# Source order on three engines in a decoder layer: a scan over time laid out as a pipeline by hand

## The chip, the cores and the metric

The kernel runs on one core of a Trainium2 chip. The metric is the device time of one execution in microseconds (us), as a median over runs. The engines are named as in the profile: PE (TensorE, matmuls), PEld (its weight loads), DVE (VectorE), ACT (ScalarE), POOL (GpSimd) and SP (SyncE, whose queue issues most DMAs).

## The reference, cut to what matters

One decoder layer on x of shape 8 x 512 x 512, all in float32. It has three parts, each followed by a residual and a layer norm:

```python
x = layernorm(x + mamba(x))              # a selective scan over 512 time steps
x = layernorm(x + cross_attention(x, ctx))   # 16 heads of 32
x = layernorm(x + experts(x))            # 32 experts, 4 per token, and a shared one
```

The change lies in the first two parts and in the router and the shared expert. The first is, for each batch entry, 1024 channels d and 16 states n:

```python
xz = layernorm(x) @ in_proj; x_main, z = split(xz)
x_main = silu(causal_conv4(x_main))
dt, Bs, Cs = split(x_main @ x_proj); dt = softplus(dt @ dt_proj + b)
h[t] = exp(A * dt[t]) * h[t-1] + dt[t] * Bs[t] * x_main[t]     # for each d, n
y[t] = sum_n h[t] * Cs[t] + x_main[t] * D
out = res_scale * (y * silu(z)) @ out_proj + x
```

## The kernel before, in words

`program` (L1433) runs three stages after each other: `layers` (L83), `experts` (L1136) and `finish` (L1388). Only `layers` is touched.

**The scan.** Each of the 8 batch entries ("batches") is cut into two chunks of 256 time steps. A chunk is worked off in 32 steps; step k takes one block of 128 channels (8 blocks, two to a pair) and one group of 4 of the 16 states. So there are 64 steps a batch and 512 in all. A step does this:

- `carry` (L448, ACT): takes an `h` tile of 128 x 4 x 257 from a ring of four and copies the last state of the chunk before into its first column (L452).
- `decays` (L442, ACT): four exponentials into one of two `da` tiles (L446). They are issued one step ahead.
- `scan` (L455, DVE): the product dt·x·B into `h` (L458), the scan itself (L462), and in the first chunk a copy of the last state (L464).
- `collect` (L466): the product of `h` with C on DVE (L479), and four matmuls on PE (L483) that sum the states into `py`; the first group of a block adds x·D by two more matmuls (L471). There is one `py` tile (pool `psy`, one buffer), which holds a pair of blocks.
- `gated` (L491, DVE): every eighth step, multiplies a finished `py` by silu(z) (L495).

B and C are spread over partitions by DMAs (`bcast`, L380) from a scratch tensor, dt and dt·x by DMAs in `prepare` (L393).

**Side work.** Between the steps the loop issues other work. The front of the next chunk: `load_x`, `norm_x`, `flip_x`, `convolve` (L320), `x_proj` (L365), `gate_x` (L353), and `prepare` for each pair. The back of the last chunk: `twice_x` (L497) and `back` (L502, two halves of matmuls with out_proj, then a layer norm). And the attention, router and shared expert of the batch before: `units` (L715) and `sources` (L663) give a list of small pieces with weights in us, and the loop takes from the list in step with a planned budget (`work`, L1023). A piece issues its PE work and returns its consumers as a function; `do` (L1014) issues a piece and then, by `settle` (L1005), the consumers of the piece before; `dry` issues all that are left. The attention's pieces are `maximum` (score product, then the reduce `mx` on DVE, L777), `weigh` (score product, then an exponential on ACT, L805) and `gather` (L817). Score products share two PSUM buffers (pool `pss`), nearly all other PE results two more (pool `psm`, tag `mm`).

**What sets the order.** The source gives an order, but a list scheduler lays out each engine's instructions anew, by its own estimates of time, wherever dependences allow. It holds for all engines; only the silu calls and their table loads are held in program order (L359).

Of the kernel before, what the change touches and what calls it, by code (L numbers as in the profile page):

```python
# [8 lines left out]
F32 = mybir.dt.float32  # L9
# [3 lines left out]
ALU = mybir.AluOpType  # L13
# [4 lines left out]
P = 128  # L18
# [6 lines left out]
NST = 16  # L25
RANK = 32
CC = DI // P
T = 256
NT_ = T // P
NG = 4  # L30
HP = P // 2
# [51 lines left out]
def layers(ctx, tc, a, x1d, filld, based, xbuf):  # L83
# [23 lines left out]
    nc = tc.nc  # L107
# [11 lines left out]
    psy = ctx.enter_context(tc.tile_pool(name="l_psy", bufs=1, space=PSUM))  # L119
# [239 lines left out]
    def silu(*tiles):  # L359

        for v in tiles:
            tc.keep_in_program_order(nc.scalar.activation(v, v, AF.Silu))
        tc.keep_in_program_order(nc.scalar.preload_act_table_set(LN_EXP))
# [78 lines left out]
    def decays(c, g, dt, da):  # L442

        for n in range(NG):
            j, m = n // 2, n % 2
            nc.scalar.activation(da[:, n, 1:], dt[:, c % 2, j, :], AF.Exp, scale=aneg[:, c, j, g, m : m + 1])  # L446

    def carry(t, c, g):  # L448

        last = state[:, c, g].unsqueeze(2)  # L450
        h = mp.tile([P, NG, T + 1], F32, tag="h", name="h", bufs=4)
        nc.scalar.copy(h[:, :, 0:1], last if t else nothing)  # L452
        return h
# [9 lines left out]
        if t < S // T - 1:  # L463
            nc.vector.tensor_copy(state[:, c, g].unsqueeze(2), h[:, :, T : T + 1])  # L464

    def collect(c, g, h, bc, py, f):  # L466


        if g == 0:
            for j in range(2):  # L470
                nc.tensor.matmul(  # L471
                    py[j * HP : (j + 1) * HP, c % 2, :],
                    ident[:, j * HP : (j + 1) * HP],
                    f["xs"][c // 2][:, c % 2, :],
                    start=(c % 2 == 0),
                    stop=False,
                )
        steps = h.rearrange("p (j m) t -> p j m t", j=2)[:, :, :, 1:]
        nc.vector.tensor_tensor(steps, steps, bc[1], ALU.mult)  # L479
        for m in range(NG // 2):  # L480
            for j in range(2):
                s = (g, m, c % 2)
                nc.tensor.matmul(  # L483
                    py[j * HP : (j + 1) * HP, c % 2, :],
                    twice,
                    h[:, j * 2 + m, 1:],
                    start=False,
                    stop=(s == (NST // NG - 1, NG // 2 - 1, 1)),
                )

    def gated(q, f, py):  # L491

        f["xs"].pop(q)
        pair = f["zs"][:, 2 * q : 2 * q + 2, :]
        nc.vector.tensor_tensor(pair, pair, py, ALU.mult)  # L495

    def twice_x(b, t, f):  # L497
        f["o"] = o = mp.tile([P, NT_, D], F32, tag="xt", name="o")
        nc.sync.dma_start(o, a["x"][b, t * T : (t + 1) * T, :].rearrange("(j p) d -> p j d", p=P))
        nc.scalar.mul(o, o, 2.0)  # L500
# [31 lines left out]
    def load(name):  # L532
        loaded[name] = w = p2.tile([P, DC, D], F32, tag="wa", name="wa")
        nc.sync.dma_start(w, rows(a[name]))
# [479 lines left out]
    def do(fn, *args, first=False):  # L1014

        if first:
            dry()
        rest = fn(*args)
        settle()
        if rest:  # L1020
            left.append(rest)

    def work(k):  # L1023

        front = 6.9 if k in (1, 2) else 3.4 if 3 <= k < 7 or k in (12, 15, 18, 21, 24) else 1.0 if k in (11, 26) else 0.0
        return 1.2 + front

    f = {"xt": x0}
# [12 lines left out]
    bc, n = bcast(f, 0), 0  # L1041
    nc.scalar.activation(aneg, aneg, AF.Exp)
    nc.vector.tensor_scalar(aneg, aneg, -1.0, None, ALU.mult)
    decays(0, 0, f["ready", 0][0], das[0])
    old, side, cleared = None, [], 0

    for i, (b, t) in enumerate(chunks):
        nf = {}
        after = chunks[i + 1] if i + 1 < len(chunks) else None
        if t == 0:  # L1050
            side, spent = units(b - 1) if b else sources(0), 0.0

            own = [work(k) for k in range(len(steps))] * 2
            whole = sum(own) + sum(x[0] for x in side)
        py = None
        for k, (q, g, ci) in enumerate(steps):
            if ci == 0:
                if (q, g) != (CC // 2 - 1, NST // NG - 1):
                    bcn = bcast(f, (g + 1) % (NST // NG))
                else:  # L1060
                    bcn = bcast(nf, 0) if after else None
            h = carry(t, 2 * q + ci, g)

            if k + 1 < len(steps) or after:
                nq, ng, ni = steps[(k + 1) % len(steps)]
                decays(2 * nq + ni, ng, (f if k + 1 < len(steps) else nf)["ready", nq][0], das[(n + 1) % 2])
            scan(t, 2 * q + ci, g, f["ready", q][1], bc, das[n % 2], h)
            n += 1
            if k % 8 == 0:
                if k:  # L1070
                    gated(q - 1, f, py)
                elif old:
                    gated(CC // 2 - 1, old[2], old[3])
                py = psy.tile([P, 2, T], F32, tag="py", name="py")
            if i == 0 and k == 0:
                load("Wo")
            if i == 0 and k == 2:
                biases()
            if k == 0 and old:
                twice_x(*old[:3])  # L1080
            if k in (1, 2) and old:
                do(back, k - 1, *old[:3], first=True)
            if 3 <= k < 7:
                do(gate_x, k - 3, f, first=(k == 3))
            if k == 7:
                dry()
                silu(f["zs"])
            if k % 8 == 3:
                if q + 1 < CC // 2:
                    do(prepare, q + 1, f)  # L1090
                elif after:
                    do(prepare, 0, nf)
            if after:
                if k == 5:
                    load_x(*after, nf)
                if k == 9:
                    norm_x(nf)
                if k == 11:
                    for j in range(DC // 2):
                        do(flip_x, j, nf)  # L1100
                if k in (12, 15, 18, 21):
                    do(convolve, after[1], (k - 12) // 3, nf, first=(k == 12))
                if k == 23:
                    dry()
                    silu(*nf["xs"].values())
                if k == 24:
                    do(x_proj, nf)
            if side and (k >= 3 or t and k == 0):
                at = t * len(steps) + k + 1
                while side and spent + sum(own[:at]) <= whole * at / len(own):  # L1110
                    w, fn, alone = side.pop(0)
                    spent += w
                    do(fn, first=alone)
            settle()
            collect(2 * q + ci, g, h, bc, py, f)
            if ci == 1:
                bc = bcn
            while i < 2 and cleared < E * (i * len(steps) + k - 6) // (2 * len(steps) - 7):
                clear(cleared)
                cleared += 1  # L1120
        while t and side:
            _, fn, alone = side.pop(0)
            do(fn, first=alone)
        old = (b, t, f, py)
        f = nf
    gated(CC // 2 - 1, old[2], old[3])
    twice_x(*old[:3])
    for j in range(2):
        do(back, j, *old[:3], first=True)
    dry()  # L1130
    for _, fn, alone in units(B - 1):
        do(fn, first=alone)
# [300 lines left out]
def program(tc, a, out):  # L1433
    nc = tc.nc
    with tc.tile_pool(name="dram", bufs=1, space=DRAM) as dram:
        x1d = dram.tile([N, D], F32, name="x1d")
        filld = dram.tile([B, S], F32, name="filld")

        based = dram.tile([N + P, D], F32, name="based")
        xbuf = dram.tile([SLOTS, ROW], F32, name="xbuf")  # L1440
        nc.scalar.preload_act_table_set(LN_EXP)

        with ExitStack() as ctx:
            layers(ctx, tc, a, x1d, filld, based, xbuf)
        with ExitStack() as ctx:
            experts(ctx, tc, a, xbuf, based)
        with ExitStack() as ctx:
            finish(ctx, tc, based, out)
# [31 lines left out]
```

## Time and profile before

| | us |
|---|---|
| median of 3 runs | 5548.85 (5548.56 to 5548.85) |
| the profiled execution | 5555.79 |
| its span, first to last instruction | 5554.1 |
| busy in the span: PE, DVE, ACT | 4883.9, 4349.2, 2592.8 |
| first scan of the kernel, last scan | 56.6, 3680.6 |
| batch 0 (its 64 steps) | 365.2 |
| batches 1 to 6, each | 466.6 to 470.2 |
| from the last scan to the experts' first product | 268 |
| experts, finish | 1533, 70 |

The span is that of one execution under the profiler; the median is of executions that were only timed. The profile's columns: busy time is the time in which an engine has an instruction at work; "idle before" is the idle time just ahead of an instruction, and the name behind the arrow is what ended it. A line number is that of the kernel before. PE counts are of the profile's records, two for each float32 matmul of the source. The whole page has a view of the chain that ended last; here it shows only the last 100 us, the experts' last write and `finish`, and says nothing on the stage in question.

### The profile page before, as it was taken

The page shows a single profiled execution, that of the slowest core. Times are in us where ns is not written, and L with a number is a line of the kernel's source. Part 1 is how long each engine was busy: PE and PEld are TensorE (multiplying, and loading weights), DVE is VectorE, ACT ScalarE, POOL GpSimd, SP SyncE. Part 2 cuts the span into 40 slices and gives each one's busy share as a digit, 9 for nine tenths or more (in the row PEclk, how much of TensorE's full clock was granted, in tenths as well). Part 3 has the DMA queues.
Part 4 walks back from the last instruction along what each step waited for, and adds up shares of the span by engine and source line. Part 5 has one row for each costly group of instructions (what it writes and reads, how often), then busy time and mean ns, then how long its engine had stood idle before and what let it go on. Part 6 is the DMA issues. An engine that isn't in the chain of part 4 may idle for free. (4 is left out here: it accounts for less than half of the span.)

```text
span 5554.1 us, 60352 instructions
## 1 busy us (share of the span) xinstructions
PE 4883.9 (88%) x19752; PEld 2720.5 (49%) x19752; DVE 4349.2 (78%) x5738; ACT 2592.8 (47%) x5483; POOL 560.9 (10%) x424
## 2 busy tenths in 40 slices
PE   6768889888988988888888898879899999999994
PEld 3334344334434434443443343333577777777773
DVE  7998989989889989899989999864466565555554
ACT  5554565655556555555555655523222222222223
POOL 1000002002000200200010020010111111111111
PEclk7878999999999999999999999989999999999997
DMA  6887345445534634544463464441345444454444
GB/s 183 246 239 203 108 130 184 114 120 154 167 104 113 203 92 129 184 123 113 124 199 104 114 193 110 113 157 44 102 121 125 125 125 124 121 126 124 115 121 146
DMA packets 554282, 769.83 MB, mean 139 GB/s; under 512 B 135754, under 2 KB 268394, under 8 KB 551920
## 3 DMA queue, kind: packets, MB, share of 16 engines
q1 hardware_dynamic: 517952, 677.55, 41.5%
q0 software_dynamic: 33280, 76.90, 7.3%
q10 hardware_dynamic: 2736, 11.54, 0.5%
q8 instruction: 156, 2.56, 0.2%
q14 instruction: 158, 1.29, 0.1%
HBM read 508.68 MB, written 165.05 MB: 121 GB/s over the span
## 5 line engine op out<-in xcount | busy, mean ns | idle before, releaser
L446 ACT ACTIVATE l_da<-both,l_aneg 128x256 f32<-128x256 f32 x2048 | 888.7, 499 | 791.5 <-DVE h L462 744.2
L462 DVE TENSOR_TENSOR_SCAN h<-l_da,h 128x1028 f32<-128x1028 f32 x512 | 1169.4, 2291 | 49.9 <-ACT h L452 27.3
L483 PE MATMUL py<-h,l_twice 128*64 128x256 f32 x4096 | 632.0, 424 | 194.2 <-DVE h L479 194.0
L458 DVE TENSOR_TENSOR h<-both,bc 128x1024 f32<-128x1024 f32 x512 | 617.5, 1213 | 141.8 <-PE py L483 78.2
L479 DVE TENSOR_TENSOR h<-h,bc 128x1024 f32<-128x1024 f32 x512 | 621.9, 1218 | 6.3 <-DMA l_qa<-l_ka 0.3
L483 PEld LDWEIGHTS py<-h,l_twice 128*64 128x64 f32 x4096 | 295.2, 148 | 570.5 <-issue 246.4
L775 PE MATMUL ps_s<-l_ka,l_qa 64*128 64x512 f32 x1024 | 315.2, 695 | 141.9 <-DVE mx L777 141.4
L1230 PE MATMUL ps_h<-xT,w 128*128 128x320 f32 x1536 | 435.6, 433 | 0.0
L1310 POOL DMA_INDIRECT based<-y,xe x160 | 251.2, 1570 | 1313.4 <-ACT y L1333 573.4
L1251 DVE TENSOR_TENSOR hT<-ps_h,p 128x320 f32<-128x320 f32 x128 | 62.9, 491 | 379.1 <-PE ps_h L1230 379.1
L777 DVE TENSOR_REDUCE mx<-ps_s 128x2 f32<-128x1024 f32 x256 | 310.2, 1215 | 56.2 <-PE ps_s L775 55.5
L1230 PEld LDWEIGHTS ps_h<-xT,w 128*128 128x128 f32 x1536 | 292.2, 190 | 118.2 <-issue 0.4
L801 PE MATMUL ps_t<-l_qa,l_ka 64*128 64x512 f32 x1024 | 300.6, 651 | 15.0 <-ACT eT L805 11.4
L805 ACT ACTIVATE eT<-ps_t 128x1024 f32<-128x1024 f32 x256 | 258.7, 1012 | 109.2 <-PE ps_t L801 108.7
L817 PE MATMUL po<-eT,l_va 128*64 128x512 f32 x1024 | 281.5, 628 | 24.6 <-ACT raw L829 20.8
L650 POOL DMA_INDIRECT xbuf<-x2t,dest x128 | 218.7, 1708 | 815.8 <-DVE dest L644 777.4
L1230 PE MATMUL ps_h<-t,s 128*128 128x320 f32 x1024 | 286.1, 432 | 0.0
L712 PE MATMUL ps_p<-x2T,wa 128*128 128x512 f32 x512 | 247.5, 633 | 11.8 <-DVE hT L892 10.3
L311 PE MATMUL ps_z<-xnT,wm 128*128 128x256 f32 x1024 | 241.0, 389 | 17.8 <-DVE o L521 17.0
L311 PE MATMUL ps_x<-xnT,wm 128*128 128x256 f32 x1024 | 242.5, 390 | 2.9 <-DMA wm<-in_in_proj_w 2.0
L512 PE MATMUL po<-wm,zs 128*128 128x512 f32 x512 | 234.6, 608 | 3.9 <-DMA wm<-in_out_proj_w 1.8
L1230 PEld LDWEIGHTS ps_h<-t,s 128*128 128x128 f32 x1024 | 194.6, 190 | 81.1
(234 smaller groups left out, 7414.6 us busy)
## 6 DMA issues: line engine op xcount, KB each, us to landing
bc<-scr SPq DMA_DIRECT2D x1024, 128.0 KB
w<-in_w SPq DMA_DIRECT2D x93, 1024.0 KB
wm<-in_in_proj_w SPq DMA_DIRECT2D x128, 512.0 KB
xbuf<-zero SPq DMA_DIRECT2D x32, 1362.5 KB
xe<-xbuf SPq DMA_DIRECT2D x32, 1362.5 KB
both<-dt SPq DMA_DIRECT2D x256, 128.0 KB
both<-dtx SPq DMA_DIRECT2D x256, 128.0 KB
wm<-in_out_proj_w SPq DMA_DIRECT2D x64, 512.0 KB
```

The source lines that it names most:

```text
L311: nc.tensor.matmul(ps[:, i, :], w[:, dc, i * P : (i + 1) * P], f["xnT"][:, dc, :], start=(dc == 0), stop=(dc == DC - 1),)
L446: nc.scalar.activation(da[:, n, 1:], dt[:, c % 2, j, :], AF.Exp, scale=aneg[:, c, j, g, m : m + 1])
L458: nc.vector.tensor_tensor(steps, dtx[:, c % 2].unsqueeze(2).to_broadcast([P, 2, NG // 2, T]), bc[0], ALU.mult)
L462: nc.vector.tensor_tensor_scan(flat, da.rearrange("p n t -> p (n t)"), flat, 0.0, ALU.mult, ALU.add)
L479: nc.vector.tensor_tensor(steps, steps, bc[1], ALU.mult)
L483: nc.tensor.matmul(py[j * HP : (j + 1) * HP, c % 2, :], twice, h[:, j * 2 + m, 1:], start=False, stop=(s == (NST // NG - 1, NG // 2 - 1, 1)),)
L775: nc.tensor.matmul(ps[:, j, :], qa[r, lt * P : (lt + 1) * P], ka[r, :], start=True, stop=True)
L777: return lambda: nc.vector.tensor_reduce(mx[:, lt, :].unsqueeze(2), ps, AX.X, ALU.max) and None
L801: nc.tensor.matmul(ps[:, j, :], ka[r, kc * P : (kc + 1) * P], qa[r, :], start=True, stop=True)
L805: nc.scalar.activation(eT, ps, AF.Exp)
L817: nc.tensor.matmul(po[j * 2 * HD : (j + 1) * 2 * HD, :], va[:, kc, i, j * HD : (j + 2) * HD], eT[:, j, :], start=(kc == 0), stop=(kc == SC ...
L1230: nc.tensor.matmul(ps, w[:, n, r * P : (r + 1) * P], x[:, n, :], start=not more and n == 0, stop=n == 1, skip_group_check=more,)
```

## The change

It does four things, all in `layers`.

1. `manual_schedule` for ACT, DVE and PE: inside `layers` these three engines keep the order of the source. POOL and SP, and with SP the DMAs, are still laid out by the scheduler. 
2. `collect` keeps only the DVE product with C. Its matmuls become a function, `products`, which the loop calls at the end of the next step. `py` is taken in `products`, and `gated` moves from step k % 8 == 0 to k % 8 == 1.
3. `carry` for step k+1 is issued in step k, ahead of the decays for step k+1.
4. A `settle()` stands right after each step's scan, so that a consumer left over from one step follows the next step's scan. It replaces the one before `collect`. `back`, `gate_x` and the silu of z move one step later, and `work`'s budget with them.

```diff
-    def collect(c, g, h, bc, py, f):
-        if g == 0:
-            for j in range(2):
-                nc.tensor.matmul(py[...], ident[...], f["xs"][c // 2][:, c % 2, :], ...)
+    def collect(c, g, h, bc, f):
         steps = h.rearrange("p (j m) t -> p j m t", j=2)[:, :, :, 1:]
         nc.vector.tensor_tensor(steps, steps, bc[1], ALU.mult)
-        for m in range(NG // 2):
-            ...
+        xs = f["xs"][c // 2]
+        def products():
+            if g == 0 and c % 2 == 0:
+                f["py"] = psy.tile([P, 2, T], F32, tag="py", name="py")
+            py = f["py"]
+            ...
+        return products
...
     decays(0, 0, f["ready", 0][0], das[0])
+    ahead, products = carry(0, 0, 0), None
...
-            h = carry(t, 2 * q + ci, g)
+            h = ahead
             if k + 1 < len(steps) or after:
                 nq, ng, ni = steps[(k + 1) % len(steps)]
+                ahead = carry(t if k + 1 < len(steps) else after[1], 2 * nq + ni, ng)
                 decays(...)
             scan(t, 2 * q + ci, g, f["ready", q][1], bc, das[n % 2], h)
             n += 1
-            if k % 8 == 0:
-                if k:
-                    gated(q - 1, f, py)
+            if k % 8 == 1:
+                if k > 1:
+                    gated(q - 1, f)
                 elif old:
-                    gated(CC // 2 - 1, old[2], old[3])
-                py = psy.tile([P, 2, T], F32, tag="py", name="py")
+                    gated(CC // 2 - 1, old[2])
...
             if k == 0 and old:
-                twice_x(*old[:3])
-            if k in (1, 2) and old:
-                do(back, k - 1, *old[:3], first=True)
-            if 3 <= k < 7:
-                do(gate_x, k - 3, f, first=(k == 3))
-            if k == 7:
+                twice_x(*old)
+            settle()
+            if k in (2, 3) and old:
+                do(back, k - 2, *old, first=True)
+            if 4 <= k < 8:
+                do(gate_x, k - 4, f, first=(k == 4))
+            if k == 8:
                 dry()
                 silu(f["zs"])
...
-            if side and (k >= 3 or t and k == 0):
+            if side and (k >= 4 or t and k < 2):
...
-            settle()
-            collect(2 * q + ci, g, h, bc, py, f)
+            if products:
+                products()
+            products = collect(2 * q + ci, g, h, bc, f)
...
         with ExitStack() as ctx:
+            ctx.enter_context(tc.manual_schedule(engines={mybir.EngineType.Activation, mybir.EngineType.DVE, mybir.EngineType.PE}))
             layers(ctx, tc, a, x1d, filld, based, xbuf)
```

More of the change, by code (lines that the diff above doesn't have):

```diff
@@ L464, in scan, with gated @@
             nc.vector.tensor_copy(state[:, c, g].unsqueeze(2), h[:, :, T : T + 1])
-    def collect(c, g, h, bc, py, f):
-        if g == 0:
-            for j in range(2):
[L471 to L477, printed above, removed]
+    def collect(c, g, h, bc, f):
         steps = h.rearrange("p (j m) t -> p j m t", j=2)[:, :, :, 1:]
         nc.vector.tensor_tensor(steps, steps, bc[1], ALU.mult)
-        for m in range(NG // 2):
[L481 to L491, printed above, removed]
+        xs = f["xs"][c // 2]
[3 more added lines that the diff above has]
+            py = f["py"]
+            if g == 0:
+                for j in range(2):
+                    nc.tensor.matmul(
+                        py[j * HP : (j + 1) * HP, c % 2, :],
+                        ident[:, j * HP : (j + 1) * HP],
+                        xs[:, c % 2, :],
+                        start=(c % 2 == 0),
+                        stop=False,
+                    )
+            for m in range(NG // 2):
+                for j in range(2):
+                    s = (g, m, c % 2)
+                    nc.tensor.matmul(
+                        py[j * HP : (j + 1) * HP, c % 2, :],
+                        twice,
+                        h[:, j * 2 + m, 1:],
+                        start=False,
+                        stop=(s == (NST // NG - 1, NG // 2 - 1, 1)),
+                    )
+        return products
+    def gated(q, f):
         f["xs"].pop(q)
         pair = f["zs"][:, 2 * q : 2 * q + 2, :]
-        nc.vector.tensor_tensor(pair, pair, py, ALU.mult)
+        nc.vector.tensor_tensor(pair, pair, f["py"], ALU.mult)
     def twice_x(b, t, f):
@@ L1023, in work @@
     def work(k):
-        front = 6.9 if k in (1, 2) else 3.4 if 3 <= k < 7 or k in (12, 15, 18, 21, 24) else 1.0 if k in (11, 26) else 0.0
+        front = 6.9 if k in (2, 3) else 3.4 if 4 <= k < 8 or k in (12, 15, 18, 21, 24) else 1.0 if k in (11, 26) else 0.0
         return 1.2 + front
@@ L1054, in layers @@
             whole = sum(own) + sum(x[0] for x in side)
-        py = None
         for k, (q, g, ci) in enumerate(steps):
@@ L1123, in layers @@
             do(fn, first=alone)
-        old = (b, t, f, py)
+        old = (b, t, f)
         f = nf
-    gated(CC // 2 - 1, old[2], old[3])
-    twice_x(*old[:3])
+    products()
+    gated(CC // 2 - 1, old[2])
+    twice_x(*old)
     for j in range(2):
-        do(back, j, *old[:3], first=True)
+        do(back, j, *old, first=True)
     dry()
```

## The prediction

> **What bounds the kernel now.** I read three views, in this order. First the busy time by stage, cut at the first scan of a batch (times from the timeline). The columns are the stretch, its length, then the busy time of PE, its weight loads, DVE, ACT and POOL with their counts, the granted clock, the DMA share and GB/s.
>
> ```profile
> 56.60:421.80 365.20, 243.50 (x990) 127.11 (x988) 343.31 (x350) 198.61 (x466) 20.98 (x12) 0.76 0.81 237
> 1359.00:1827.40 468.40, 412.26 (x1685) 194.71 (x1684) 425.99 (x500) 267.87 (x564) 41.86 (x29) 0.94 0.48 138
> 3233.10:3683.00 449.90, 386.93 (x1580) 177.41 (x1579) 402.25 (x432) 241.45 (x516) 34.09 (x21) 0.93 0.46 134
> 3683.00:3951.00 268.00, 226.99 (x735) 92.80 (x736) 106.67 (x207) 65.51 (x86) 31.84 (x35) 0.89 0.33 113
> 3951.00:5484.00 1533.00, 1532.31 (x6259) 1131.45 (x6257) 895.15 (x1609) 425.52 (x929) 246.59 (x157) 1.00 0.47 116
> ```
>
> These are batch 0, batch 3 (batches 1 to 6 all take 467 to 470), batch 7, the last attention unit alone, and the experts. The change touches all but the last. In batch 3 DVE is busy for 426.0 of 468.4 us (91%) and PE for 412.3 (88%): two engines close together, and only 42.4 us of DVE idle that any order of instructions could win back. Second, DVE's groups in batch 3, with the idle time ahead of each and what ended it.
>
> ```profile
> L462 DVE TENSOR_TENSOR_SCAN h<-l_da,h 128x1028 f32<-128x1028 f32 x64 | 146.5, 2292 | 6.6 <-ACT h L452 3.8 <-ACT l_da L446 0.7
> L479 DVE TENSOR_TENSOR h<-h,bc 128x1024 f32<-128x1024 f32 x64 | 77.9, 1219 | 0.9
> L458 DVE TENSOR_TENSOR h<-both,bc 128x1024 f32<-128x1024 f32 x64 | 77.4, 1213 | 18.4 <-PE py L483 11.1 <-DMA both<-dtx 7.3
> L777 DVE TENSOR_REDUCE mx<-ps_s 128x2 f32<-128x1024 f32 x32 | 38.7, 1214 | 2.1 <-PE ps_s L775 2.0
> L345 DVE SCALAR_TENSOR_TENSOR xs<-xp,l_cw,xs 128x256 f32<-128x256 f32 x48 | 20.6, 479 | 5.5 <-ACT xs L337 5.2
> ```
>
> The three instructions of a step cost 4.7 us; 64 steps give 302 of the 426 us. The named waits are small and spread out: an h buffer not yet free (11.1), a copied dt late (7.3), a convolution (5.5). Third, the timeline of DVE, for what lies between two instructions (start, duration).
>
> ```profile
> 3560.15 2.30 DVE L462 TENSOR_TENSOR_SCAN h<-l_da,h 128x1028 f32<-128x1028 f32 x1
> 3562.49 1.23 DVE L479 TENSOR_TENSOR h<-h,bc 128x1024 f32<-128x1024 f32 x1
> 3563.63 1.22 DVE L777 TENSOR_REDUCE mx<-ps_s 128x2 f32<-128x1024 f32 x1
> 3564.76 0.68 DVE L418 SCALAR_TENSOR_TENSOR dtx<-dtx,u 128x512 f32<-128x512 f32 x1
> ```
>
> L479 reads what the scan wrote and starts 0.04 after the scan's end. L777 needs nothing of L479 and starts 0.09 before its end. Over all neighbours in the trace less than 0.35 us apart, an independent one starts 0.081 us before the end (median), a dependent one 0.034 after it, and a scan straight after its own product L458 0.103 after. So which instructions are neighbours has a price.
>
> [...]
>
> **The change, part by part.** All per batch of 64 steps, against batch 3.
>
> *Source order on DVE.* It removes no instruction: both built programs have 498 a batch, whose mean durations sum to 450.4 us. Before, 144 of the neighbours are dependent: 34 are pairs of taps, which overlap all the same, 21 are product and scan, 89 others. 450.4 − 388×0.081 + 21×0.103 + 89×0.034 = 424.2, against 426.0 measured, so the counting holds. After, the built order has 288: product, scan and copy now always stand together. 40 pairs of taps and 7 of reduces overlap; 64 are product and scan; 177 others: 450.4 − 257×0.081 + 64×0.103 + 177×0.034 = 442.2. So **+18 us on the engine that sets the pace**. What the source order may still lose to waits before it is slower: 468.4 − 442.2 = 26 us, 0.41 us a step.
>
> *Products a step later, carries a step sooner.* PE no longer stands behind the DVE product of its own step (10.1 us of PE's idle time in this batch). The carry of step k+1 needs the products of step k−3, which PE issues in step k−2, with four h buffers as before; so the 11.1 us at L458 and most of the 6.6 at the scan go. A carry that still waits for PE now holds up, behind it in ACT's queue, the four decays of that step and every evacuation after them, and so PE's next buffers; with a step and a half of slack I cost that at nothing, and at up to 3 us a batch around `back` if the slack is gone. `gated` waits for the products of the step before and holds PE's next products until it is done: counted in the next item. Next late is whatever consumer waits for PE.
>
> *Consumers behind the next scan.* I laid PE's and DVE's sums of each step (built order times the durations above) side by side. With PE's side work due 1.2 us before DVE ends the step, its products waiting for DVE's previous step, and for `gated` every eighth (one py buffer), PE is late by **12 us** in all, mostly around `back` (two pieces of some 7 us in steps 2 and 3); without any lateness 0, with PE never ahead of the scan 27.
>
> *Reduces.* Seven steps hold two neighbouring `mx` reduces with a `weigh` between their products. The two score buffers then alternate, so the second product waits for the first reduce, and DVE for it: in the tail the trace shows this gap as 1.42 us. Before, the scheduler put other work there (2.1 us in all). 7×1.42 = **10 us**; low 3 if PE finds the other buffer, high 13.
>
> *Chains across engines in one step*, which the scheduler filled: norm, transposes, shared hidden product, projection and taps in steps 52 to 54 (PE's three pieces, 3.5+3.5+3.1, end some 5 us after DVE wants the taps); `prepare` at step 11 (1.5); the second `output` (1.5); x1 fetched row block by row block in step 13 (3). Sum **11 us**; low 3, high 20, as the trace doesn't show this order.
>
> *DMAs.* SP's and POOL's queues aren't in the manual schedule; SP's order changes with the simulated one, the count (3189) doesn't; the loads of B and C wait there for the collecting product, which ends its step as before. `prepare` now stands five steps before its use; of 7.3 us of dt waits I keep **2** (0 to 9).
>
> *ACT.* Table loads fall from 18 to 10 a batch, 8×1.283 = 10 us; but ACT is busy 268 of 468 and works a step ahead, so nothing on the path. If ACT became late it would cost at most these 10 back.
>
> Sum: 442 + 12 + 10 + 11 + 2 = 477, of which I take off 1 for lateness counted twice: **476, +7.6 us a batch**, 46 for batches 1 to 6. Batch 0 has no attention: the same counting gives a floor of 363.5 where it was 341.6, and I leave it 12 of its 22 idle us (DMA share 0.81 there): 376, +11 (the biases' matmuls of step 2, now in DVE's order, are some 3 of these). Batch 7 and the last unit together: +6 (its floor is up 18 too; the unit alone has PE in the same forced order, 85% busy, and DVE at 40%; hence nothing). Experts and finish: their sources and built order are unchanged, 0. Sum +63. The profiled execution took 5555.79 (span 5554.1), the median is 5548.85, 0.12% below; the sum on the median gives **5612**.
>
> **Rivals.**
>
> *The pipeline works (ends faster).* One mechanism: PE has a step's lead (its side work of step k may start after the products of step k−2, some 3.5 us before DVE's consumers of step k), and this covers reduces and chains too. Then a batch takes 442 + 12 + 2 = 456: 7×(−12) and nothing for batch 0 gives **5465**. For it: named waits at L458 go, ACT is ahead. Against it: 26 us is all there is, and pairs of reduces can't be covered with two buffers. It decides where waits are under 0.41 us a step.
>
> *Step by step.* PE's lead is eaten by its buffers (two mm, two score, one py), so each step costs the larger of PE's and DVE's sums: these maxima sum to 475, and reduces and chains come on top, 21: 496 a batch, 7×28 + 15 gives **5760**. For it: PE 88% busy. Against: ACT frees most mm buffers early.
>
> *They cancel.* 468 to 470 a batch, **5550**. That the change doesn't do what it says is excluded: the built order shows it.
>
> **How the numbers follow.** Forecast 0.53, faster rival 0.26, step by step 0.12, cancelling 0.09. The forecast's own range, with the bounds of reduces, chains and DMA (−19 to +19 a batch about 476, not all at one end), is 5540 to 5690. For 8 in 10 I take 5465 to 5725. 0.2% (11 us) is about what a measurement of this kernel can tell from no change. Faster by more: 0.27; within: 0.08; slower: 0.65.
>
> **What would show it.** DVE busy in a batch near 442, against 426: then the counting of neighbours is right. DVE waits at `mx` near 10 us a batch with PE's score product as releaser; waits at L458 for `py` near nothing; table loads 10 a batch; a wait for taps or x2 around steps 52 to 54. A batch under 460 makes me wrong on the waits; one over 490 says PE sets the pace.

## The result, and the profile after

The changed kernel takes 5966.6 us (5961.25 to 5970.12, four runs) against 5548.85: ratio 1.075, 95% interval 1.0731 to 1.0769. The forecast had the sign and the place, but a seventh of the size: +63 us forecast, +418 measured. The time lies outside the range.

First the same stages as before, cut at the first scan of batches 0, 3 and 7, at the last scan, and at the experts' first product (columns: stretch, length, busy time of PE, PEld, DVE, ACT, POOL, granted clock, DMA share, GB/s).

```profile
57.10:449.10 392.00, 252.21 (x1010) 138.21 (x1012) 362.39 (x355) 194.42 (x468) 5.12 (x12) 0.76 0.72 213
1498.20:2023.90 525.70, 428.92 (x1684) 200.91 (x1684) 440.38 (x498) 258.04 (x556) 29.51 (x30) 0.88 0.42 124
3600.80:4101.00 500.20, 404.32 (x1584) 184.27 (x1584) 421.01 (x457) 235.35 (x509) 24.00 (x20) 0.88 0.41 119
4101.00:4368.00 267.00, 218.67 (x725) 89.86 (x726) 105.12 (x185) 67.65 (x89) 24.22 (x27) 0.89 0.31 103
```

From first scan to first scan, batch 0 takes 392.0 us (365.2 before), batches 1 to 6 523 to 526 (467 to 470), batch 7 497.8 to its last scan (447.4); what follows the last scan takes 1866.9 (1873.5). So +27, +340, +50 and -7, which is the 411 by which the spans differ (5965.5 against 5554.1). Batch 3 shows two things at once. DVE's busy time rose by 14.4 us for the same 498 instructions, the way the counting of neighbours had it (+18). And its idle time doubled, from 42.4 to 85.3 us, where it was to fall to 34. PE's idle time rose with it, from 56 to 97 us.

DVE's groups in batch 3 (instructions, busy time and mean, idle time just ahead and what ended it):

```profile
L462 DVE TENSOR_TENSOR_SCAN h<-l_da,h 128x1028 f32<-128x1028 f32 x64 | 147.2, 2300 | 6.6 <-ACT l_da L446 1.6
L469 DVE TENSOR_TENSOR h<-h,bc 128x1024 f32<-128x1024 f32 x64 | 78.0, 1218 | 0.6
L458 DVE TENSOR_TENSOR h<-both,bc 128x1024 f32<-128x1024 f32 x64 | 77.9, 1217 | 0.0
L785 DVE TENSOR_REDUCE mx<-ps_s 128x2 f32<-128x1024 f32 x32 | 38.8, 1217 | 15.8 <-PE ps_s L783 15.8
L345 DVE SCALAR_TENSOR_TENSOR xs<-xp,l_cw,xs 128x256 f32<-128x256 f32 x48 | 22.5, 482 | 14.8 <-ACT xs L337 13.6
```

The scan's own three instructions run as long as before, and L458, with 18.4 us of idle time ahead of it before, has none. That part of the pipeline works. (Of the 6.6 us ahead of L462, 1.6 are a wait; the rest is the small gap of some 0.08 us between L458 and the scan that depends on it, in each of 64 steps.) What waits now is the side work. DVE's waits in the same batch (us in total, times, longest):

```profile
DVE mx L785 <- PE ps_s L783: 15.8, 11, 3.8
DVE o L529 <- PE po L520: 14.8, 4, 7.2
DVE xs L345 <- ACT xs L337: 13.6, 3, 8.6
DVE dtx L418 <- ACT dtx L414: 9.5, 5, 3.4
DVE total L856 <- ACT r L855: 7.0, 2, 6.5
DVE zs L503 <- PE py L489: 3.6, 1, 3.6
```

None of these lines is the scan, whose one wait for decays is 1.6 us. Each is a consumer that stands at a fixed place in DVE's order, while its operand comes late from PE or ACT. (L785 is L777 of before, L529 is `norm`, L418 `prepare`, L856 the sum of `output`, L503 `gated`.) PE stands in the same way, in the same batch:

```profile
PE ps_tr L886 <- ACT x2t L80: 13.8, 1, 13.8
PE ps_p L720 <- DVE attT L858: 11.1, 1, 11.1
PE ps_t L809 <- DVE mx L785: 10.2, 3, 3.6
PE py L479 <- ACT l_da L446: 8.9, 1, 8.9
```

One account serves for all that follows. I split DVE's time in batch 3 into the durations of its 498 instructions, the sum of the small gaps between neighbours (under 0.35 us; negative where neighbours overlap), and the longer gaps, called waits.

| batch 3, us | length | durations | small gaps | waits |
|---|---|---|---|---|
| before | 468.4 | 454.0 | -22.4 | 36.8 |
| after | 525.7 | 456.0 | -2.9 | 72.6 |
| difference | +57.3 | +2.0 | +19.5 | +35.8 |

The forecast had +18 for neighbours, and 35 for all waits (12 for PE's lateness, 10 for reduces, 11 for chains, 2 for DMAs), about what the kernel before has. So the first difference is right, and the waits are twice what was forecast. The level that the forecast built on was low as well: its 442.2 us for durations and small gaps compares with 456.0 - 2.9 = 453.1, and the 424.2 of before with 454.0 - 22.4 = 431.6. The prediction took its 424.2 as confirmed by the 426.0 of busy time, but busy time leaves out the short idle gaps that the counting holds.

### The profile page after: what moved, and what is told of

Same layout as the page of the kernel before. It is cut to its first block, busy times and chain, and to the rows that moved or that the text cites. A ratio compares the mean times of both kernels' runs of the same rounds, so it can differ in the third digit from the quotient of the medians.

```text
span 5965.5 us, 60313 instructions
## 1 busy us (share of the span) xinstructions
PE 4998.5 (84%) x19752; PEld 2763.4 (46%) x19752; DVE 4468.2 (75%) x5738; ACT 2521.8 (42%) x5428; POOL 485.6 (8%) x424
## 5 line engine op out<-in xcount | busy, mean ns | idle before, releaser
L462 DVE TENSOR_TENSOR_SCAN h<-l_da,h 128x1028 f32<-128x1028 f32 x512 | 1177.3, 2299 | 56.2 <-ACT l_da L446 14.8
L446 ACT ACTIVATE l_da<-both,l_aneg 128x256 f32<-128x256 f32 x2048 | 872.4, 498 | 444.7 <-DVE h L462 442.4
L489 PE MATMUL py<-h,l_twice 128*64 128x256 f32 x4096 | 617.8, 425 | 128.5 <-DVE h L469 128.4
L469 DVE TENSOR_TENSOR h<-h,bc 128x1024 f32<-128x1024 f32 x512 | 624.0, 1219 | 5.6
L458 DVE TENSOR_TENSOR h<-both,bc 128x1024 f32<-128x1024 f32 x512 | 623.4, 1218 | 6.4 <-DMA bc<-scr 6.4
L489 PEld LDWEIGHTS py<-h,l_twice 128*64 128x64 f32 x4096 | 288.7, 148 | 495.3 <-issue 215.2
L785 DVE TENSOR_REDUCE mx<-ps_s 128x2 f32<-128x1024 f32 x256 | 310.1, 1217 | 151.8 <-PE ps_s L783 151.6
L825 PE MATMUL po<-eT,l_va 128*64 128x512 f32 x1024 | 288.9, 644 | 22.4 <-ACT raw L837 17.9
L720 PE MATMUL ps_p<-x2T,wa 128*128 128x512 f32 x512 | 286.9, 717 | 12.7 <-DVE hT L900 8.0
L311 PE MATMUL ps_z<-xnT,wm 128*128 128x256 f32 x1024 | 256.2, 407 | 25.2 <-ACT dt L409 16.9
L345 DVE SCALAR_TENSOR_TENSOR xs<-xp,l_cw,xs 128x256 f32<-128x256 f32 x384 | 180.0, 482 | 108.9 <-ACT xs L337 99.2
L658 POOL DMA_INDIRECT xbuf<-x2t,dest x128 | 180.6, 1411 | 899.5 <-DVE dest L652 356.7
L311 PE MATMUL ps_x<-xnT,wm 128*128 128x256 f32 x1024 | 247.4, 396 | 0.6 <-ACT xnT L300 0.5
L311 PEld LDWEIGHTS ps_z<-xnT,wm 128*128 128x128 f32 x1024 | 202.3, 203 | 82.0 <-ACT dt L409 21.0
```

The source lines that it names most:

```text
L311: nc.tensor.matmul(ps[:, i, :], w[:, dc, i * P : (i + 1) * P], f["xnT"][:, dc, :], start=(dc == 0), stop=(dc == DC - 1),)
L458: nc.vector.tensor_tensor(steps, dtx[:, c % 2].unsqueeze(2).to_broadcast([P, 2, NG // 2, T]), bc[0], ALU.mult)
L462: nc.vector.tensor_tensor_scan(flat, da.rearrange("p n t -> p (n t)"), flat, 0.0, ALU.mult, ALU.add)
L489: nc.tensor.matmul(py[j * HP : (j + 1) * HP, c % 2, :], twice, h[:, j * 2 + m, 1:], start=False, stop=(s == (NST // NG - 1, NG // 2 - 1, 1)),)
L720: nc.tensor.matmul(ps, lhs(dc), rhs(dc), start=(dc == 0), stop=(dc == DC - 1))
L785: return lambda: nc.vector.tensor_reduce(mx[:, lt, :].unsqueeze(2), ps, AX.X, ALU.max) and None
```

## The experiments

My theory after the result: a few late places (`back`, the reduces, `prepare`, the taps) hold DVE, and each can be mended alone. The rival: orders fixed on DVE and on PE make the two stand at each other by turns, so that mending one place moves the wait to the next. A third: the layout is itself worse, whoever orders it. The kernel before, timed again with each group of experiments, had medians from 5549 to 5557 us, so a difference of less than some 10 us between two experiments says nothing by itself. Every kernel is the changed one with the edit shown, unless said otherwise; ratios are to the kernel before, with 95% intervals; "waits" and "small gaps" are those of batch 3 as above.

**The layout without the fixed order, and the fixed order without the layout.**

```diff
-            ctx.enter_context(tc.manual_schedule(engines={Activation, DVE, PE}))   # e1: taken out
```

> The changed source without the manual schedule: the list scheduler lays out all engines again. If in-order waits on DVE and adjacent dependent neighbours are the cause (+36 and +20 us in a batch of 526), both go and a batch takes 460 to 475, in all 5500 to 5600 us. If it is the reshaped source itself (products a step later, work shifted), it stays over 5800.

```diff
+            ctx.enter_context(tc.manual_schedule(engines={Activation, DVE, PE}))   # e2: put into the kernel before
```

> The source of before with the manual schedule alone, products and consumers in the same step. In-order waits: DVE's product with C is now followed by consumers with no scan between, PE has no step of lead, so slower than the changed kernel, 6200 to 6800 us. If the reshaping did nothing for the in-order engines, it is within 1% of 5967.

Measured: 5607.5 us, 1.0097 (1.0077 to 1.0116), for the layout alone, and 6660.1 us, 1.1991 (1.1971 to 1.2011), for the fixed order alone. In batch 3 the layout under the scheduler has small gaps of -21.1 and waits of 43.4; the fixed order of the old source -2.3 and 166.8. So the layout does what it is laid out for: it takes 694 us off a kernel whose engines keep the source's order. But it doesn't pay for that order: under the scheduler it costs 1% rather than gain, and the fixed order costs 359 us more.

**Which engine's order.**

```diff
-            ctx.enter_context(tc.manual_schedule(engines={Activation, DVE, PE}))
+            ctx.enter_context(tc.manual_schedule(engines={DVE}))   # e3; e4 {Activation, PE}; e16 {PE}; e17 {Activation}; e18 {DVE, PE}
```

> Changed source, only DVE in source order, PE and ACT by the scheduler. If DVE's own order is the cause, nearly all of the loss stays: 5850 to 6000 us. If PE's order sets the pace, it falls to 5600 to 5700.

> Changed source, ACT and PE in source order, DVE by the scheduler. If DVE's own order is the cause: 5550 to 5700 us, with overlap of neighbours back near -22 us a batch and waits below 50. If PE's order sets the pace, 5850 to 6000.

> Changed source, PE alone in source order, ACT and DVE by the scheduler. With ACT and PE in order it was 5821, with none 5607. If PE's order is what blocks, 5750 to 5820; if ACT's (decays behind evacuations that wait for PE), 5620 to 5680.

> The changed source with only ACT in the order of the source. If each fixed order costs by itself and the three overlap (5607 with none, 5777 with PE alone, 5859 with DVE alone, 5821 with ACT and PE, 5967 with all), ACT alone costs about the difference between ACT with PE and PE alone, 44: 5650 (5620 to 5680). If ACT's queue is what ties DVE to PE (a carry that waits for PE holds up the decays behind it), ACT alone costs most of what two engines cost: over 5730.

> The changed source with DVE and PE in the order of the source and ACT laid out by the scheduler. If the loss lies between DVE and PE and ACT only adds its own small share, 5920 (5890 to 5950), all but some 45 of the whole. If ACT's fixed order is what ties the two together, the time falls near that of DVE alone, below 5870.

| engines in the source's order | us | ratio | small gaps | waits | PE idle |
|---|---|---|---|---|---|
| none (e1) | 5607.5 | 1.0097 (1.0077 to 1.0116) | -21.1 | 43.4 | 64.0 |
| ACT (e17) | 5658.2 | 1.0191 (1.0174 to 1.0208) | -25.8 | 56.3 | 57.9 |
| PE (e16) | 5777.1 | 1.0392 (1.0375 to 1.0410) | -19.6 | 64.3 | 84.5 |
| ACT, PE (e4) | 5820.8 | 1.0474 (1.0452 to 1.0495) | -22.5 | 71.2 | 89.2 |
| DVE (e3) | 5859.1 | 1.0552 (1.0534 to 1.0571) | -4.6 | 59.2 | 87.3 |
| DVE, PE (e18) | 5961.4 | 1.0736 (1.0719 to 1.0754) | -3.8 | 70.0 | 100.9 |
| all (after) | 5966.6 | 1.0750 (1.0731 to 1.0769) | -2.9 | 72.6 | 96.8 |

The small gaps close only where DVE is in order, by 16.5 us a batch for DVE alone: that is the neighbours' price by itself. The waits grow with any of the engines. With DVE and PE fixed the time is that of all three within some 5 us: ACT's order adds nothing to theirs, and my e18 forecast (ACT adds some 45) was too high for ACT. But the loss doesn't need both. DVE alone costs 252 us over e1 and PE alone 170, which sum to more than the 354 of the two together; so the costs overlap, and each order makes waits even where the other engine is free (59.2 and 64.3, from 43.4). Neither of e4's branches came true (5821, between them). Where the waits stand depends on which order is fixed. With PE alone fixed, the scheduler lets DVE run ahead until it needs an h buffer that PE has not yet read:

```profile
DVE h L458 <- PE py L489: 35.9, 13, 13.4
```

With DVE fixed as well this line is gone, and DVE stands at the side work instead:

```profile
DVE xs L345 <- ACT xs L337: 18.4, 5, 9.9
DVE o L529 <- PE po L520: 13.2, 4, 7.2
DVE dtx L418 <- ACT dtx L414: 12.9, 3, 4.5
DVE mx L785 <- PE ps_s L783: 7.5, 7, 1.6
```

**The neighbours alone.** DVE's product with C of step k-1 is put between L458 and the scan of step k, so that the scan no longer stands right behind the product that it reads, nor the product with C right behind its scan.

```diff
-    def scan(t, c, g, dtx, bc, da, h):
+    def scan(t, c, g, dtx, bc, da, h, between=None):
...
+        if between:
+            between()
...
-            scan(t, 2 * q + ci, g, f["ready", q][1], bc, das[n % 2], h)
+            scan(t, 2 * q + ci, g, f["ready", q][1], bc, das[n % 2], h, weighted)
```

> Changed kernel with DVE's product with C of step k-1 put between the product and the scan of step k, so that no scan stands straight behind its own product. Neighbour theory: 64 pairs become independent, 64 x 0.184 = 12 us a batch plus up to 5 where collect stood behind its scan; waits unchanged; 90 to 130 us faster, near 5860. If neighbours cost nothing[...], 5967 within 20.

Measured: 5906.5 us, 1.0637 (1.0620 to 1.0655). Small gaps fall from -2.9 to -14.5, waits stay (74.9). The timeline shows where (start, duration):

```profile
1722.26 1.22 DVE L458 TENSOR_TENSOR h<-both,bc 128x1024 f32<-128x1024 f32 x1
1723.39 1.22 DVE L474 TENSOR_TENSOR h<-h,bc 128x1024 f32<-128x1024 f32 x1
1724.53 2.29 DVE L464 TENSOR_TENSOR_SCAN h<-l_da,h 128x1028 f32<-128x1028 f32 x1
```

L474 (the product with C) starts 0.09 us before L458 ends, and the scan 0.08 before L474 ends. In the changed kernel the scan stands right behind its own product and starts 0.10 after its end, while an instruction of other data behind the scan starts 0.07 before its end:

```profile
2006.26 1.22 DVE L458 TENSOR_TENSOR h<-both,bc 128x1024 f32<-128x1024 f32 x1
2007.58 2.30 DVE L462 TENSOR_TENSOR_SCAN h<-l_da,h 128x1028 f32<-128x1028 f32 x1
2009.81 0.66 DVE L914 TENSOR_TENSOR z<-ps_p,x2t 128x512 f32<-128x512 f32 x1
```

So an exchange of neighbours alone gives back 60 us of the 418. The small gaps gained what was forecast (11.6 us a batch, of 12); the time gained less (60 us, of 90 to 130).

**Mending single places.** `prepare` a step later (e5); the other taps of a convolution one `settle` later (e6); the fourth convolution a step sooner (e12); `gated` ahead of its step's product and scan (e10).

```diff
-            if k % 8 == 3:
+            if k % 8 == 4:  # e5
...
-            return other_taps
+            return lambda: other_taps            # e6
...
-                if k in (12, 15, 18, 21):
-                    do(convolve, after[1], (k - 12) // 3, nf, first=(k == 12))
+                if k in (12, 15, 18, 20):        # e12
+                    do(convolve, after[1], (k - 11) // 3, nf, first=(k == 12))
...
-            scan(t, 2 * q + ci, g, f["ready", q][1], bc, das[n % 2], h)     # e10: moved
-            n += 1
             if k % 8 == 1:
                 ...
+            scan(t, 2 * q + ci, g, f["ready", q][1], bc, das[n % 2], h)
+            n += 1
```

> Changed kernel with prepare one step later (k % 8 == 4), so that at steps 3 and 35 the norm of back no longer has to run before prepare's matmuls, but follows the next scan. If the waits come from the distance between producer and consumer in the source: the 15 us a batch ahead of L529 fall to below 5, and the kernel gains 50 to 90 us. If PE's pace costs the time, the wait reappears behind other consumers and the kernel stays within 20 us of 5967.

> Changed kernel with the convolution's other taps issued one piece later. Distance theory: of 13.6 us a batch ahead of L345 (4.2 at step 16, 8.6 at step 54) most goes, 50 to 90 us in all. PE's pace: within 20 us of 5967.

> Changed kernel with the fourth convolution of the next chunk at k = 20 instead of 21, so that at step 52 its projection stands ahead of the transposes of x2 in PE's queue, where they wait 13.8 us for the layer norm. Head-of-line theory: the 8.6 us ahead of the taps at step 54 fall below 2, 30 to 50 us in all. If PE's work alone counts, the wait reappears at the router's or another consumer and the gain is under 15 us.

> Changed kernel with gated ahead of its step's product and scan instead of behind them (still k % 8 == 1), so that the one py buffer comes free 3.5 us sooner. Head-of-line theory: PE idles 8.9 us at step 1 behind the first products of a new pair, with back's ready matmuls queued behind them; the same at each of 8 pairs a batch. Then waits ahead of L529 fall by 3 to 7 us a batch, and all by 8 to 15: 60 to 110 us faster. If PE's total work sets the pace, or py comes free in time, within 20 us of 5967.

Measured: 5945.0 us, 1.0707 (1.0689 to 1.0725), for e5; 5968.0, 1.0746 (1.0728 to 1.0764), for e6; 5963.3, 1.0740 (1.0722 to 1.0757), for e12; 6029.8, 1.0859 (1.0841 to 1.0877), for e10. Only e5 gains, by 22 us, where 50 to 90 were forecast if single places were at fault. e6 says nothing: the taps stayed the first work behind the scan, with the same wait of 8.6 us at step 54. In e12 that wait is gone, others of 7.6 and 5.0 us for the same operand stand at steps 20 and 52, and the waits ahead of the taps are longer in all (13.6 in the changed kernel):

```profile
DVE xs L345 <- ACT xs L337: 17.8, 3, 7.6
```

At `mx` they are shorter (15.8 to 7.6), so that all waits come to 69.7. In e5 the 14.8 us ahead of L529 fall to 5.2, and those ahead of L418 rise from 9.5 to 20.7:

```profile
DVE dtx L418 <- ACT dtx L414: 20.7, 7, 6.2
...
DVE o L529 <- PE po L520: 5.2, 4, 2.3
```

The place for e10 I took from the timeline of the changed kernel, around the first `gated` of a chunk:

```profile
1505.66 0.68 DVE L503 TENSOR_TENSOR zs<-zs,py 128x512 f32<-128x512 f32 x1
...
1506.49 1.12 PE L479 MATMUL py<-xs,l_ident 128*64 128x256 f32 x4 [8.94 <-ACT l_da L446]
...
1507.37 1.95 PE L489 MATMUL py<-h,l_twice 128*64 128x256 f32 x8
...
1509.24 7.30 PE L520 MATMUL po<-wm,zs 128*128 128x512 f32 x16
...
1523.38 0.75 DVE L529 SCALAR_TENSOR_TENSOR o<-po,l_rs,o 128x512 f32<-128x512 f32 x1 [7.16 <-PE po L520]
```

PE is idle for 8.94 us and starts again 0.15 after `gated` has ended (the single `py` must be read first; the decay that the profile names as releaser ends at that moment, but these matmuls don't read it). Behind it stand both halves of `back`, 7.3 and 7.1 us, and at their end DVE, at `norm`, for 7.16. With `gated` sooner, DVE waits less at L529 but stands at `gated` for the last products:

```profile
DVE zs L503 <- PE py L489: 18.6, 5, 7.3
...
DVE o L529 <- PE po L520: 10.6, 4, 4.6
```

15.0 us more there against 4.2 less, and the kernel is 63 us slower where 60 to 110 were to be gained. In e5 and e10 the wait that grew is that of the very piece that the edit moved, so these two show that a place can't be shifted for nothing, not that a wait wanders elsewhere. Last, e9, e10 and e12 together (their three edits in one):

> Interleaved product with C, gate first and project first together. Head-of-line theory: the gains add, 60 + 60 to 110 + 40: 5750 to 5810 us, still slower than before. If the waits only move about, 5880 to 5910, the interleaving alone.

Measured: 6058.5 us, 1.0905 (1.0887 to 1.0924). Small gaps stay mended (-14.4), and waits are 97.8: more than with any of the three alone (74.9, 77.7 and 69.7), and 25 more than in the changed kernel, where the three changes taken singly sum to some 5. So places can't be mended one by one and their gains added. That some choice of mends helps is not excluded: e10 was already a loss by itself, and e5, which gained, was not in this kernel.

**Less work for PE.** Every second matmul with `twice` (L489) is left out, so half of the states are missing from y.

```diff
-            for m in range(NG // 2):
+            for m in (NG // 2 - 1,):
```

> Changed kernel that leaves out half of the py matmuls (two of four in each step, so half of the states are missing from y). It takes some 0.6 us of PE work out of each step, 36 us a batch, and leaves DVE's and ACT's order. If PE's pace sets the time: 250 to 300 us faster, near 5700. If it is the latency of chains at some places: under 120 us, at 5850 or above.

Measured: 5870.3 us, 1.0570 (1.0552 to 1.0587). PE's busy time in batch 3 falls by 29.9 us (428.9 to 399.1), and the batch by 14.0. A microsecond of PE work is worth about half a microsecond, so PE isn't the bound by its sum; its idle time rose to 112.7.

**The distance of products and carries.** The products in their own step again (e19, e19b), two steps later (e21, with the gate, `back` and `gate_x` one step later too), and the carry in its own step (e20).

```diff
-            if products:
-                products()
-            products = collect(2 * q + ci, g, h, bc, f)
+            collect(2 * q + ci, g, h, bc, f)()                      # e19, e19b
...
+            if len(products) == 2:                                  # e21
+                products.pop(0)()
+            products.append(collect(2 * q + ci, g, h, bc, f))
...
-            h = ahead
+            h = carry(t, 2 * q + ci, g)                             # e20
...
-                ahead = carry(t if k + 1 < len(steps) else after[1], 2 * nq + ni, ng)
```

> The changed kernel with one of its parts undone: the products follow their own step's product with C again, and the gate stands in every eighth step's place of before. If the later products are what the pipeline lives on, PE now stands behind DVE's product in every step and most of the 694 us between the source of before in fixed order (6660) and the changed one (5967) comes back: over 6300. If PE's lead is eaten by its buffers anyway, the products' place matters little: below 6100.

> The changed kernel with the products at the end of their own step, and the gate, every eighth step, right ahead of the product with C there (in the run labelled e19_products_now it stood ahead of silu(z) once a chunk). The run before took 6140, and this one only mends the place of the gate, so 6100 to 6160 if it is the products that cost; under 6020 if it was the gate's place.

> The changed kernel with the products two steps later than their product with C instead of one, and with them the gate, back and gate_x one step later (and the prepare of step 3 in step 4). If DVE waits for PE because PE's side work is held behind products that are not ready, the second step of slack takes a good part of DVE's waits at mx, o and xs: below 5900. If PE's lead is bounded elsewhere (by two score buffers, two mm buffers, and the places where one engine's piece needs the other's latest result), nothing is gained: 5940 to 6010.

> The changed kernel with the other part undone: the carry is issued in its own step again, behind the decays of the step before. If ACT works a step ahead, little changes: 5967 to 6010. If the sooner carry is what keeps DVE's product of dt, x and B from waiting for its h buffer, waits of at least 1 us a step appear ahead of L458 or the scan: over 6200.

In e19 the gate stood ahead of silu(z) once a chunk, so that one pair of blocks was multiplied by z itself; e19b has it behind. Measured: 6139.9 us, 1.1055 (1.1037 to 1.1074), for e19 and 6164.1, 1.1092 (1.1073 to 1.1110), for e19b; 6220.9, 1.1193 (1.1175 to 1.1212), for e21; 5999.1, 1.0804 (1.0786 to 1.0822), for e20. So neither side of the distance is free. With none, PE stands at DVE's product, as the wait of e19b shows (6.4 us in 3 waits in the changed kernel):

```profile
PE py L489 <- DVE h L469: 64.9, 27, 10.8
```

With two, PE holds each h tile a step longer, and by the waits the ring of four runs out: ACT, a step ahead, stands at the carry for PE's reads, and DVE at L458 for 20.9 us, where it had no wait. PE stands longer for `gated`, too:

```profile
ACT h L452 <- PE py L489: 197.7, 51, 10.9
...
PE py L479 <- DVE zs L503: 22.7, 3, 13.9
```

(In the changed kernel the first is 29.0 us in 13 waits, and the wait ahead of L479 is the one of 8.9.)

Both of my e21 forecasts were wrong: it is 254 us slower, and the waits point to resources that I had not counted, the h ring above all. One step is the best of the three distances tried; a larger ring, which would show whether it is the ring, wasn't. The later products are worth some 200 us of the 694 that the layout brings, the sooner carry some 32; the rest, some 460, wasn't taken apart.

None of the 18 kernels is faster than the kernel before; nearest is the layout under the scheduler, 1% slower.

## Why the prediction was right in sign and wrong in size

- *Source order on DVE, +18 us a batch*: right as a difference, +19.5 in batch 3 and 24.5 in batch 0 (22 forecast). The level was too low by 11 us a batch, as said above.
- *Products later, carries sooner*: right where it named a line. The 11.1 us at L458 for `py` and the 7.3 for the copied dt are gone. Of the 6.6 ahead of the scan, 4.5 were waits, and 1.6 of them are left; that the sum is 6.6 again comes from the small gaps. A waiting carry costs DVE next to nothing in the changed kernel, as costed: ACT waits there 13 times, 29.0 us in all, but DVE's wait for decays is 1.6, and with ACT's order free (e18) the time is the same within some 5 us.
- *PE's lateness around `back`, 12*: measured 14.8 at L529 and 3.6 at `gated`, 18.4. The place was right, the size short by a third.
- *Reduces, 10*: measured 15.8, in eleven waits where I had seven. Their mean of 1.4 us is mine only by luck: they run from under 0.4 to 3.8. My 1.42 was one gap of the tail, where most are 1.7; the two reduces of step 30 wait 1.7 each, but 6.3 us stand at the two of step 20, where PE comes out of a gap of 3.5 us and runs their products at the slow rate (four score products in 2.08 us, the next four in 1.13; last section).
- *Chains, 11*: this is the step that failed. Measured 36, three times the forecast and beyond its upper bound of 20: the taps 13.6 (5 forecast), `prepare` 9.5 (1.5), the second `output` 7.0 (1.5), layer norm, hidden products and the rest 6. The fetch of x1 (3) shows no wait. *DMAs, 2*: nothing is seen.
- *ACT's tables*: 10 a batch where it had been 18, each 1283 ns in both traces, and nothing on the path: right.
- *Batch 0, 376*: 392.0. Of its 21.1 us of waits 18.4 stayed, where I let ten go, and durations and small gaps come to 373.5, where I had 363.5. *Batch 7 and the last unit, +6*: +50 up to its last scan. *Experts and finish, 0*: right; all that follows the last scan changed by -7.

Of the 50 us by which batch 3 runs beyond the forecast's 476, the chains are 25, the level of durations and small gaps 11, `back` and the reduces 6 each. I had costed each chain by itself, with PE at its post 1.2 us before DVE, and summed. What such a sum leaves out can be read at steps 52 to 54 of batch 3. PE stands for 13.8 us at L886, for a layer norm that DVE ends and ACT scales (L80). The projection for the taps (L311) needs nothing of it, but is queued behind, and starts 13.5 us after L886; DVE then stands 8.6 us at the taps (L345). In e12, which takes the projection ahead of L886, that wait is gone. So where DVE is late with an operand of PE, PE is late with all that is queued behind, and DVE stands at one of these. That places do not add up is shown by e12 and e13. That all of the added waits are such rounds between the two engines is argued from places like this one, and not shown: of the 354 us for both, DVE's order alone makes 252 and PE's alone 170, and no experiment opens the round. (That PE's idle time rose with DVE's proves nothing, since it follows from the longer batch.)

The rival "step by step" had this direction, with 496 a batch, and by the prediction's own sign a batch over 490 says that PE sets the pace. Its mechanism, the larger of PE's and DVE's sums in each step, is not it either: the batch takes 525.7, and half of PE's work in the products, 29.9 us, is worth only 14 (e8).

What it comes to, for batch 3's +57: 19.5 for neighbours, 2 for durations, 6.6 for waits that the layout has under the scheduler too (e1), and 29 for waits that only the fixed orders bring. Open is whether some other fixed order would lose nothing, such as the one that the scheduler arrives at written out by hand, and why the layout costs 1% under the scheduler. Neither was tried further.

## What to carry to other kernels

Before engines are put in source order, count the stretch's slack on each of them: here DVE had 42 us of idle time in 468 and PE 56, and two engines near 90% that hand work to each other in both directions had no room for this hand-laid order with one step of distance. Follow a late operand through the queues of both engines before costing the waits, as a sum of chains costed one by one came to a third of what they took. Before widening the distance between producer and consumer, count the buffers that it holds. A reordering that leaves an engine's work the same can still lengthen it, by putting dependent instructions side by side (on DVE here 19.5 us a batch).

## What the runs showed of the hardware

**PE's clock follows its gaps.** PE's busy time in batch 3 rose from 412.3 to 428.9 us for the same matmuls, and the granted clock fell from 0.94 to 0.88. The timeline above shows how: behind the gap of 8.94 us, four L479 take 1.12 us and eight L489 1.95, and the granted clock from 1506.4 to 1509.3 is 0.50. Ten microseconds of work later, with the clock at 1.00 from 1510.0 to 1518.0, the same groups are

```profile
1516.48 0.65 PE L479 MATMUL py<-xs,l_ident 128*64 128x256 f32 x4
1516.96 1.03 PE L489 MATMUL py<-h,l_twice 128*64 128x256 f32 x8
```

which is close to half the time. Over batches 1 to 6 of the changed kernel, 262 of the 266 L489 that start within 6 us behind a PE gap of 3.0 us or more are slow (336 L489 last over 0.55 us, with a median of 0.63; that of the others is 0.38). Such gaps are 51 in these six batches, and behind 48 of them the granted clock is 0.50; before, there are 19. Shorter gaps show the slow rate, too: of the 228 L489 with a longest gap of 2.0 to 3.0 us in the 6 us ahead of them 74 are slow, and of the 770 with one of 0.5 to 2.0 us none. So all 336 stand behind a gap of 2.0 us or more (in the trace of before this is less sharp: 41 of the 554 behind gaps of 0.5 to 2.0 us are slow). How long it lasts: the slow L489 behind the gaps of 3.0 us or more start up to 5 us after them, and of the 692 that start 9 to 20 us after, none is slow.

My prediction left this out: a wait of PE can make its next work slower, as the L489 above show. PE's busy time in batch 3 grew by some 17 us. Over batches 1 to 6, with each matmul set against the median of its shape in the kernel before, the durations grew by 165 us in sum (they overlap, so this is more than the busy time grew by), and about three quarters of that (123) stands within 6 us behind gaps of 2.0 us or more. At e8's worth of a half, 17 us of PE work are an estimated 8 of the 57; it wasn't tried alone. PE's own order doesn't settle it by itself: with PE alone in order (e16) PE's busy time in batch 3 is 415.4, and with ACT alone (e17) 426.8.

**Dependent neighbours.** A chained pair on DVE costs 0.12 to 0.18 us more than an unchained one, by the medians in the prediction. The trace of the changed kernel has the same: the scan starts 0.102 us after its product L458 ends (median of 503), L469 0.034 after the scan that it reads (of 74), and L458 0.082 before the end of an L469 of other data (of 505). e9 shows this as time on the whole kernel: 11.6 us a batch in small gaps, 60 us in all. Why a chained pair costs more, the runs don't show.
